# Graph attention over a sparse matrix: the second part's order on three engines written out by hand, and the last tile worked in column halves

## The chip, the core and the metric

The kernel runs on one core of a Trainium2 chip. The metric is the device time of one launch in microseconds (us); lower is better. The core's engines are named as the profile names them: PE (TensorE, the matrix array), DVE (VectorE), ACT (ScalarE), POOL (GpSimd) and SP (SyncE). Each works through a queue of its own in order, and waits there for semaphores that other engines or transfers raise.

## What is computed

```python
def reference(x, adj, Wf, bf, Wg, bg, W, bW):        # x: 3327 x 1024, adj: 3327 x 3327
    h = jnp.maximum(_layernorm(x, axis=-1), 0.0)
    f, g = h @ Wf + bf, h @ Wg + bg
    e = jax.nn.relu(f @ g.T)
    attention = softmax(jnp.where(adj > 0, e, NEG), axis=1)
    return x + attention @ (h @ W + bW)
```

All values are float32. Of each row of `adj` only some are set: a row has at most 37 neighbours in this data.

## The kernel before, in words

`edge_path` never builds the full score matrix. Its **first part** (to about 250 us) reads `adj` and `x`, stores h to memory (`hd`), makes a list of neighbours for every row (`pd`, and `cd` for rows with more than 24), and multiplies the two weight matrices into one, A. It sorts the rows by their number of neighbours and cuts them into 26 tiles of 128 rows.

The **second part** handles one tile after another, in the order `ORDER`. I call a tile by its *position* in that order, 0 to 25. `CAPS` gives each tile's cap, the number of neighbours that it is worked with. By position the caps are 12, 16, 37, 25, 23, 22, 21, 21, 20, 20, 19, 19, 18, 18, 17, 17, 17, 16, 15, 15, 15, 14, 14, 13, 13, 11. For one tile:

- `turned`, `taken`, `third`, `emptied` make q = h A. PE transposes the tile's rows of h (8 transposes), ACT copies them (`hT`), PE multiplies them by A in three thirds of 342 columns (16 passes each), and ACT copies each third into `q`; before that the banks are filled with a bias row on ACT. This is done two positions ahead.
- `dot`: for each neighbour k, POOL starts an indirect gather of 128 rows of `hd` into a buffer `G` (26 buffers in turn), and DVE multiplies G by q and sums it to a score (L986, 128x1024).
- `softmax`: DVE masks the scores (L995) and takes the negated maximum (L997; L999 joins it with that of an earlier chunk). ACT takes the exp (L1002). In a second chunk ACT makes a factor `al` (L1005) and scales the sum y by it (L1011); DVE joins the denominators (L1006) and inverts (L1009).
- `combine`: y is the sum of G times its weight. Some of the G go through DVE (L1052, one sum each, 128x1024). The others are scaled on ACT (L1046) and added by PE, transposed, in a PSUM tile `yT_ps` (L1026, 8 transposes of 128x128 each); `on_tensor` says which. The first G is scaled on ACT (L1050).
- `project`: PE adds y itself transposed (8 more), ACT copies the result (`yT`), PE multiplies by W (L1068, two halves of 512 columns, 32 passes).
- `result` and `finish`: ACT scales the product (L1090), POOL gathers the rows of x onto it and writes it out. The last tile's result is scaled and added on DVE (L1084).

Tiles with a cap over 16 are worked in two chunks, the first of 10 neighbours (19 at position 2); the others in one piece. While one unit is summed, dots of the next unit run: `AHEAD` of them are issued right after `softmax`, the rest when the next unit begins. `project` of a tile is put off until the next tile's first chunk has been combined; with a next tile in one piece, it comes at once.

What sets the order: the first part stands in a block `tc.manual_schedule` that keeps DVE, ACT, PE, POOL and SP in program order. In the second part the framework's scheduler chooses each engine's order by its own estimates, and `in_line` (L864) adds edges that keep certain PE and ACT instructions behind the last ones recorded in `queue`. DVE is free, except that the last tile's dots stand behind the sums of the tile before (`behind`).

`failed` (L1113) makes a flag of the checks of the first part: a 1x1 matmul and a DVE copy (L1120, L1121); all engines load the flag (L1122) and branch on it past a dense fallback that these inputs do not need. It is called when position 23 has been projected.

Of the kernel before, what the change touches and what calls it, by code (L numbers as in the profile page):

```python
# [33 lines left out]
AHEAD = 3  # L34
# [262 lines left out]
def edge_path(ctx: ExitStack, tc: tile.TileContext, x, adj, Wf, bf, Wg, bg, W, bW, out, flag):  # L297
# [563 lines left out]
    queue = {}  # L861

    @contextmanager
    def in_line():  # L864
        with ExitStack() as both:
            for ins in queue.values():
                both.enter_context(tc.issue_after(ins.ins))
            yield


# [15 lines left out]

    one = small.tile([P, 1], FP, name="one")
    tc.keep_in_program_order(nc.scalar.activation(one, ident[:, :1], AF.Exp))

    for at in range(2):  # L890
        filled(p_q, "ps_q", vb, QB, 6 + at, True)
        filled(p_o, "ps_o", bWb, CB, at, True)
# [15 lines left out]
    def turned(s):  # L908
# [3 lines left out]
        for g in range(0, KD, 4):  # L912
            ps = p_t.tile([P, 4, P], FP, name="ps_t")
            e["ps_t"].append(ps)
            with in_line():
                for k in range(4):
                    ins = nc.tensor.transpose(ps[:, k, :], e["hp"][:, (g + k) * P : (g + k + 1) * P], ident)  # L917
            queue["pe"] = ins

    def taken(s):  # L920
        e = st[s]
        for g, ps in enumerate(e["ps_t"]):
            with in_line():
                queue["act"] = nc.scalar.copy(e["hT"][:, 4 * g : 4 * g + 4, :], ps)  # L924

    def third(s, i):
# [7 lines left out]
        with in_line():  # L934
            for k in range(KD):
                ins = nc.tensor.matmul(  # L936
                    ps[:, :QB], e["hT"][:, k, :], A_sb[:, k, o : o + QB], start=False, stop=(k == KD - 1),
                    skip_group_check=True,
                )
        queue["pe"] = ins  # L940

    def emptied(s, i):
        e = st[s]
        at = 3 * ORDER.index(s) + i
        with in_line():
            ins = nc.scalar.copy(e["q"][:, i * QB : (i + 1) * QB], e["ps_q"][i][:, :QB])  # L946
            if at + 2 < 3 * NT:
                ins = filled(p_q, "ps_q", vb, QB, at + 2)
        queue["act"] = ins
# [29 lines left out]
    def dot(s, k, behind=None):  # L979
# [5 lines left out]
        with tc.issue_after(behind.ins) if behind else ExitStack():  # L985
            nc.vector.tensor_tensor_reduce(  # L986
                junk, g, e["q"][:, :D], 1.0, e["q"][:, D : D + 1], op0=ALU.mult, op1=ALU.add,
                accum_out=e["sc"][:, k : k + 1],
            )
# [247 lines left out]
```

## Time and profile before

| | us |
|---|---|
| median of 15 runs | 1317.32 |
| lowest and highest | 1308.71 and 1325.28 |
| the profiled execution | 1313.65 |
| its span, first to last instruction | 1311.7 |
| DVE busy in the span | 1158.1 |
| PE busy in the span | 1114.8 |
| ACT busy, POOL busy | 609.8, 886.6 |
| mean granted clock of PE | 0.942 |

A row of the table of groups gives line, engine, operation, output and inputs, count, then busy time and mean ns of one, then the idle time of the engine just before these instructions and what ended most of it. A row of a timeline gives start, length, engine, line, operation, tiles and shapes, and in brackets the idle time before it with what released it. A row of the waits gives who waited for whom, the total in us, how often, and the longest. A row of the chain of waits gives start, length and what the chain ran through. An instruction's length on DVE overlaps the next one's start slightly, so steps are best read from start to start.

### The profile page before, as it was taken

The page shows a single profiled execution, that of the slowest core. Times are in us where ns is not written, and L with a number is a line of the kernel's source. Part 1 is how long each engine was busy: PE and PEld are TensorE (multiplying, and loading weights), DVE is VectorE, ACT ScalarE, POOL GpSimd, SP SyncE. Part 2 cuts the span into 40 slices and gives each one's busy share as a digit, 9 for nine tenths or more (in the row PEclk, how much of TensorE's full clock was granted, in tenths as well). Part 3 has the DMA queues.
Part 4 walks back from the last instruction along what each step waited for, and adds up shares of the span by engine and source line. Part 5 has one row for each costly group of instructions (what it writes and reads, how often), then busy time and mean ns, then how long its engine had stood idle before and what let it go on. Part 6 is the DMA issues. An engine that isn't in the chain of part 4 may idle for free.

```text
span 1311.7 us, 14316 instructions
## 1 busy us (share of the span) xinstructions
PE 1114.8 (85%) x4488; PEld 702.2 (54%) x4488; DVE 1158.1 (88%) x2205; ACT 609.8 (46%) x943; POOL 886.6 (68%) x678
## 2 busy tenths in 40 slices
PE   2799962967846899999888998999999899999995
PEld 2566641643625566556555655556555556555553
DVE  6999987686899899999999999999999999999980
ACT  5899977133206356435543354443335433333350
POOL 8999974374675777777676676766665667656611
PEclk8899985977977999999999999999999899999998
DMA  9999995886787999989888888888888788888821
GB/s 370 413 395 397 397 338 190 275 307 252 231 297 238 318 298 312 332 294 308 286 302 264 299 292 288 283 280 287 277 291 268 241 275 283 262 286 303 271 69 50
DMA packets 101802, 374.44 MB, mean 285 GB/s; under 512 B 14747, under 2 KB 18490, under 8 KB 98519
## 3 DMA queue, kind: packets, MB, share of 16 engines
q0 software_dynamic: 80624, 290.96, 66.7%
q1 hardware_dynamic: 21094, 82.49, 16.6%
q8 instruction: 37, 0.61, 0.2%
q14 instruction: 47, 0.39, 0.1%
HBM read 344.11 MB, written 29.30 MB: 285 GB/s over the span
## 4 chain that ended last, share of the span: by engine, by line
DVE 29%; issue 29%; DMA 13%; PE 11%; ACT 8%; POOL 8%; another core or an unknown queue 2%; SPq 0%; POOLq 0%; DVEq 0%; ACTq 0%
DVE G L1052 12%; DVE cand L482 6%; POOL G L356 5%; DVE junk L986 5%; DMA G<-hd,pi 5%; PE ps_o L1068 4%; ACT G L1046 4%; PE yT_ps L1026 4%; DMA xt<-in_x_dram 3%; PE ps_q L936 3%; DMA G<-hd,perm 2%; POOL r L419 1%; DVE sc L986 1%; DVE held L493 1%
## 5 line engine op out<-in xcount | busy, mean ns | idle before, releaser
L356 POOL DMA_INDIRECT G<-hd,pi x454 | 538.1, 1185 | 206.1 <-issue 102.3
L986 DVE CUSTOM_DVE_ANT_0 junk<-G,q 128x1024 bf16<-128x1024 f32 x468 | 601.4, 1285 | 35.5 <-DMA G<-hd,pi 15.8
L1052 DVE SCALAR_TENSOR_TENSOR G<-G,sc 128x1024 f32<-128x1024 f32 x275 | 353.8, 1287 | 32.1 <-ACT G L1011 15.7
L1068 PE MATMUL ps_o<-W_sb,yT 128*128 128x512 f32 x832 | 364.0, 595 | 6.2 <-ACT yT L1060 6.2
L936 PE MATMUL ps_q<-A_sb,hT 128*128 128x342 f32 x1152 | 345.0, 454 | 9.5 <-issue 9.5
L936 PEld LDWEIGHTS ps_q<-A_sb,hT 128*128 128x128 f32 x1152 | 215.6, 191 | 117.5 <-issue 14.9
L1026 PE MATMUL yT_ps<-ident,G 128*128 128x128 f32 x1544 | 205.7, 285 | 85.7 <-ACT G L1046 61.9
L1068 PEld LDWEIGHTS ps_o<-W_sb,yT 128*128 128x128 f32 x832 | 157.7, 190 | 200.8 <-issue 188.5
L1026 PEld LDWEIGHTS yT_ps<-ident,G 128*128 128x128 f32 x1544 | 178.6, 147 | 116.2 <-ACT G L1046 74.8
L419 POOL TENSOR_TENSOR r<-r,iotaj 128x1664 f32<-128x1664 f32 (+3 forms) x50 | 183.8, 3726 | 12.5 <-ACT r L412 12.5
L1046 ACT ACTIVATE G<-G,sc 128x1024 f32<-128x1024 f32 x167 | 182.4, 1142 | 0.0
L1002 ACT ACTIVATE sc<-sc,nm 128x10 f32<-128x10 f32 (+11 forms) x41 | 12.5, 304 | 342.7 <-DVE nm L999 252.1
L552 PE MATMUL ps_A<-WgT,WfT 128*128 128x342 f32 x432 | 130.9, 462 | 2.5 <-ACT WfT L547 2.5
L482 DVE MAX8 cand<-r 128x8 f32<-128x208 f32 (+2 forms) x416 | 119.1, 360 | 4.1 <-POOL r L419 3.3
L552 PEld LDWEIGHTS ps_A<-WgT,WfT 128*128 128x128 f32 x432 | 81.9, 193 | 43.1 <-ACT WfT L547 2.6
L946 ACT COPY q<-ps_q 128x342 f32<-128x342 f32 x72 | 31.4, 437 | 155.3 <-PE ps_q L936 114.3
L412 ACT ACTIVATE r<-r 128x3327 f32<-128x3327 int32 (+3 forms) x27 | 77.3, 2863 | 8.1 <-DMA r<-in_adj_dram 8.1
L1102 POOL DMA_INDIRECT out_dram<-res,perm x25 | 31.9, 1276 | 65.2 <-DMA res<-in_x_dram,perm 61.0
L356 POOL DMA_INDIRECT res<-in_x_dram,perm x25 | 41.9, 1674 | 47.0 <-ACT res L1090 37.9
L924 ACT COPY hT<-ps_t 128x512 f32<-128x512 f32 x48 | 25.4, 581 | 75.7 <-PE ps_t L917 55.1
L356 POOL DMA_INDIRECT pi<-pd,perm x26 | 29.0, 1116 | 34.7 <-DMA cd<-cand 17.7
L536 PE MATMUL ps_tr<-ident,A_sb 128*128 128x128 f32 x128 | 22.5, 334 | 27.5 <-DMA A_sb<-in_L_gnn_Wg_dram 23.5
(139 smaller groups left out, 713.3 us busy)
## 6 DMA issues: line engine op xcount, KB each, us to landing
r<-in_adj_dram SPq DMA_DIRECT2D x24, 1663.5 KB, 12.2
xt<-in_x_dram SPq DMA_DIRECT2D x25, 512.0 KB, 12.9
hd<-xt SPq DMA_DIRECT2D x25, 512.0 KB, 10.5
G<-hd,pi POOLq DMA_INDIRECT x454
A_sb<-in_L_gnn_Wg_dram SPq DMA_DIRECT2D x8, 512.0 KB, 17.3
A_sb<-in_L_gnn_Wf_dram SPq DMA_DIRECT2D x8, 512.0 KB, 11.4
W_sb<-in_L_gnn_W_dram POOLq DMA_DIRECT2D x1, 4096.0 KB
cd<-cand SPq DMA_DIRECT2D x25, 64.0 KB, 11.8
```

What stands on the lines that cost most here:

```text
L356: return nc.gpsimd.indirect_dma_start(out=to, out_offset=None, in_=table, in_offset=bass.IndirectOffsetOnAxis(ap=idx, axis=0), **kw,)
L412: nc.scalar.activation(r[:n, b:e], a[:n, b:e], AF.Sign, accum_out=to)
L419: eng.tensor_mul(r[:n, b:e], r[:n, b:e], iotaj[:n, b:e])
L482: nc.vector.max(cands[t][:n, s * 8 : s * 8 + 8], r[:n, s * SW : min(N, (s + 1) * SW)])
L552: nc.tensor.matmul(ps[:, :QB], WfTs[c][:, k, :], WgT[:, k, o : o + QB], start=(k == 0), stop=(k == KD - 1))
L936: ins = nc.tensor.matmul(ps[:, :QB], e["hT"][:, k, :], A_sb[:, k, o : o + QB], start=False, stop=(k == KD - 1), skip_group_check=True,)
L986: nc.vector.tensor_tensor_reduce(junk, g, e["q"][:, :D], 1.0, e["q"][:, D : D + 1], op0=ALU.mult, op1=ALU.add, accum_out=e["sc"][:, k : k ...
L1026: ins = nc.tensor.matmul(e["yT"][:, c, :], g[:, c * P : (c + 1) * P], ident, is_transpose=True, start=(first and c % 4 == 0), stop=(last a ...
L1046: queue["act"] = nc.scalar.activation(g, g, AF.Copy, scale=p)
L1052: e["summed"] = nc.vector.scalar_tensor_tensor(y, g, p, y, op0=ALU.mult, op1=ALU.add)
L1068: ins = nc.tensor.matmul(ps, yT[:, k, :], W_sb[:, k, o * CB : (o + 1) * CB], start=False, stop=(k == KD - 1), skip_group_check=True,)
L1102: ins = nc.gpsimd.indirect_dma_start(out=out[:, :], out_offset=bass.IndirectOffsetOnAxis(ap=perm[:, s : s + 1] if s < N // P else final, a ...
```

## The change

The scheduler's choice in the second part is replaced: the whole second part stands in a `manual_schedule` block for ACT, DVE and PE, so each of these engines runs its instructions in program order; POOL and SP are still scheduled. `in_line`, `queue` and `behind` go.

The program order itself is new. After `softmax` of a unit come `AHEAD` = 2 dots of the next unit (none after positions 0 and 1), then `totalled` (the denominators and the inverse, formerly in `softmax`). In `combine` every DVE sum is followed by one dot of the next unit while there are any (`between`); after position 24's sums none is. Remaining dots come when the next unit begins. On ACT the factor `al` now comes ahead of the exp, and y is scaled within `softmax`, ahead of `emptied(…, 2)`, the copy of the last third of a coming q. Position 24 gives PE three of its G instead of six, position 25 five instead of four. `failed` keeps its place in the program, behind `project` of position 23; the flag is loaded after the last but one result's write.

The last tile goes through the new `ended`: its G for PE are scaled and transposed; then, for each half of 512 columns, DVE scales the first G and adds the others (six instructions of 128x512), PE adds this half of y transposed, ACT copies the half, and PE runs the half of the W product that reads it.

```diff
 LARGEST = 16
-AHEAD = 3
+AHEAD = 2
 LAG = 2
...
-    queue = {}
-
-    @contextmanager
-    def in_line():
-        with ExitStack() as both:
-            for ins in queue.values():
-                both.enter_context(tc.issue_after(ins.ins))
-            yield
-
...
-        with in_line():
-            ins = nc.scalar.copy(e["q"][:, i * QB : (i + 1) * QB], e["ps_q"][i][:, :QB])
-            if at + 2 < 3 * NT:
-                ins = filled(p_q, "ps_q", vb, QB, at + 2)
-        queue["act"] = ins
+        nc.scalar.copy(e["q"][:, i * QB : (i + 1) * QB], e["ps_q"][i][:, :QB])
+        if at + 2 < 3 * NT:
+            filled(p_q, "ps_q", vb, QB, at + 2)
...
-    def dot(s, k, behind=None):
+    def dot(s, k):
         e = st[s]
         g = G[s, k] = gpool.tile([P, D], FP, name="G")
         with tc.issue_after(st["gate"].ins) if s == ORDER[1] else ExitStack():
             st["gathered"] = gather(g, hd[:, :], e["edges"][k])
         junk = jpool.tile([P, D], BF, name="junk")
-        with tc.issue_after(behind.ins) if behind else ExitStack():
-            nc.vector.tensor_tensor_reduce(
-                junk, g, e["q"][:, :D], 1.0, e["q"][:, D : D + 1], op0=ALU.mult, op1=ALU.add,
-                accum_out=e["sc"][:, k : k + 1],
-            )
-
-    def softmax(s, k0, k1, last):
+        nc.vector.tensor_tensor_reduce(
+            junk, g, e["q"][:, :D], 1.0, e["q"][:, D : D + 1], op0=ALU.mult, op1=ALU.add,
+            accum_out=e["sc"][:, k : k + 1],
+        )
+
+    def softmax(s, k0, k1):
 
         e = st[s]
         sc = e["sc"][:, k0:k1]
         nc.vector.scalar_tensor_tensor(sc, sc, 0.0, e["mask"][:, k0:k1], op0=ALU.max, op1=ALU.add)
         nm = small.tile([P, 1], FP, name="nm")
         nc.vector.tensor_reduce(nm, sc, AX.X, ALU.max, negate=True)
+        l = small.tile([P, 1], FP, name="l")
         if k0:
             nc.vector.tensor_tensor(nm, nm, e["nm"], op=ALU.min)
-        l = small.tile([P, 1], FP, name="l")
-        with in_line():
-            nc.scalar.activation(sc, sc, AF.Exp, bias=nm, accum_out=l)
+            e["al"] = small.tile([P, 1], FP, name="al")
+            nc.scalar.activation(e["al"], e["nm"], AF.Exp, bias=nm, scale=-1.0)
+        nc.scalar.activation(sc, sc, AF.Exp, bias=nm, accum_out=l)
         if k0:
-            al = small.tile([P, 1], FP, name="al")
-            nc.scalar.activation(al, e["nm"], AF.Exp, bias=nm, scale=-1.0)
-            nc.vector.scalar_tensor_tensor(l, e["l"], al, l, op0=ALU.mult, op1=ALU.add)
+            nc.scalar.activation(e["y"], e["y"], AF.Copy, scale=e["al"])
+        else:
+            e["y"] = G[s, 0]
+            if s != ORDER[-1]:
+                nc.scalar.activation(e["y"], e["y"], AF.Copy, scale=e["sc"][:, :1])
+        e["nm"] = nm
+        e["ls"] = (e.get("l"), l)
+        e["l"] = l
+
+    def totalled(s, k0, last):
+        e = st[s]
+        if k0:
+            before, l = e["ls"]
+            nc.vector.scalar_tensor_tensor(l, before, e["al"], l, op0=ALU.mult, op1=ALU.add)
         if last:
             e["rs"] = small.tile([P, 1], FP, name="rs")
-            nc.vector.reciprocal(e["rs"], l)
-        if k0:
-            queue["act"] = nc.scalar.activation(e["y"], e["y"], AF.Copy, scale=al)
-        e["nm"], e["l"] = nm, l
+            nc.vector.reciprocal(e["rs"], e["l"])
...
 
     def on_tensor(s, k0, k1):
 
 
-        m = min(max(0, CAPS[s] - (7 if s in ORDER[-2:] else 12)), k1 - k0 - 2) if s not in ORDER[:2] else (k1 - k0) // 2
+        if s in ORDER[:2]:
+            m = (k1 - k0) // 2
+        elif s in ORDER[-2:]:
+            m = {ORDER[-2]: 3, ORDER[-1]: 5}[s]
+        else:
+            m = min(max(0, CAPS[s] - 12), k1 - k0 - 2)
         ks = range(max(k0, 1), k1)
         return [k for i, k in enumerate(ks) if (i + 1) * m // len(ks) > i * m // len(ks)]
+
+    def transposed_into(e, g, c, first, last):
+        nc.tensor.matmul(
+            e["yT"][:, c, :], g[:, c * P : (c + 1) * P], ident, is_transpose=True,
+            start=first, stop=last, skip_group_check=True,
+        )
...
-    def combine(s, k0, k1, last, ahead=None):
+            transposed_into(e, g, c, first and c % 4 == 0, last and c % 4 == 3)
+
+    def combine(s, k0, k1, last, ahead, between):
         e = st[s]
-        if not k0:
-            e["y"] = G[s, 0]
         y = e["y"]
         e["first"] = True
         pe = on_tensor(s, k0, k1) if last else []
-        for k in range(k0, k1):
+        for k in range(max(k0, 1), k1):
             p = e["sc"][:, k : k + 1]
             g = G[s, k]
             if k in pe:
                 if k == pe[-1] and ahead is not None:
                     taken(ahead)
-                with in_line() if k == pe[-1] else ExitStack():
-                    queue["act"] = nc.scalar.activation(g, g, AF.Copy, scale=p)
-                queue["pe"] = sum_transposed(e, g, e["first"], False)
+                nc.scalar.activation(g, g, AF.Copy, scale=p)
+                sum_transposed(e, g, e["first"], False)
                 e["first"] = False
-            elif k == 0:
-                queue["act"] = nc.scalar.activation(y, y, AF.Copy, scale=p)
             else:
-                e["summed"] = nc.vector.scalar_tensor_tensor(y, g, p, y, op0=ALU.mult, op1=ALU.add)
+                nc.vector.scalar_tensor_tensor(y, g, p, y, op0=ALU.mult, op1=ALU.add)
+                between()
+
+    def ended(s, k1):
+        e = st[s]
+        y = e["y"]
+        pe = on_tensor(s, 0, k1)
+        yT = yTpool.tile([P, KD, P], FP, name="yT")
+        e["yT"] = p_y.tile([P, KD, P], FP, name="yT_ps")
+        e["o"] = [banks.pop(("ps_o", OH * (NT - 1) + o)) for o in range(OH)]
+        for i, k in enumerate(pe):
+            nc.scalar.activation(G[s, k], G[s, k], AF.Copy, scale=e["sc"][:, k : k + 1])
+            for c in range(KD):
+                transposed_into(e, G[s, k], c, not i and c % 4 == 0, False)
+        for g in range(0, KD, 4):
+            half = slice(g * P, (g + 4) * P)
+            nc.vector.tensor_scalar(y[:, half], y[:, half], e["sc"][:, :1], None, op0=ALU.mult)
+            for k in range(1, k1):
+                if k not in pe:
+                    nc.vector.scalar_tensor_tensor(
+                        y[:, half], G[s, k][:, half], e["sc"][:, k : k + 1], y[:, half], op0=ALU.mult, op1=ALU.add
+                    )
+            for c in range(g, g + 4):
+                transposed_into(e, y, c, False, c % 4 == 3)
+            nc.scalar.copy(yT[:, g : g + 4, :], e["yT"][:, g : g + 4, :])
+            for o, ps in enumerate(e["o"]):
+                for k in range(g, g + 4):
+                    nc.tensor.matmul(
+                        ps, yT[:, k, :], W_sb[:, k, o * CB : (o + 1) * CB], start=False, stop=(k == KD - 1),
+                        skip_group_check=True,
+                    )
...
@@ -1119,7 +1130,6 @@
         ps = p_t.tile([P, 4, P], FP, name="ps_t")[:, 0, :]
         nc.tensor.matmul(ps[0:1, 0:1], worst, onesf, start=True, stop=True)
         nc.vector.tensor_copy(flag[0:1, 0:1], ps[0:1, 0:1])
-        return nc.values_load(flag[0:1, 0:1], min_val=0, max_val=1 << 20)
 
...
-
-                dot(s, k, st[ORDER[-2]].get("summed") if s == ORDER[-1] else None)
...
+    with tc.manual_schedule(engines={
+        mybir.EngineType.Activation, mybir.EngineType.DVE, mybir.EngineType.PE
+    }):
+        one = small.tile([P, 1], FP, name="one")
+        nc.scalar.activation(one, ident[:, :1], AF.Exp)
+        for at in range(2):
+            filled(p_q, "ps_q", vb, QB, 6 + at, True)
+            filled(p_o, "ps_o", bWb, CB, at, True)
...
+        for i, (s, k0, k1) in enumerate(units):
+            last = k1 == CAPS[s]
+            at = ORDER.index(s)
+            s2, a, b = units[i + 1] if i + 1 < len(units) else (s, 0, 0)
+            ahead = ORDER[at + 2] if last and at + 2 < NT else None
+            if at and ahead is not None:
+                fetch(ahead)
...
+            softmax(s, k0, k1)
+            if late:
+                emptied(late.pop(), 2)
+            covered = AHEAD if i > 1 else 0
+            dots(s2, range(a, min(b, a + covered)))
+            totalled(s, k0, last)
...
+            if ahead is not None:
+                turned(ahead)
+            coming = iter(range(a + covered, b) if i > 1 and s != ORDER[-2] else ())
+
+            def between(s2=s2, coming=coming):
+                for k in coming:
+                    dots(s2, [k])
+                    break
+
+            if s == ORDER[-1]:
                 result(ORDER[at - 1])
+                ended(s, k1)
                 done_with.append(ORDER[at - 1])
+                break
+            combine(s, k0, k1, last, ahead, between)
...
+                if at + 2 == NT - 1:
+                    failed()
+        finish(done_with.pop())
+        bad = nc.values_load(flag[0:1, 0:1], min_val=0, max_val=1 << 20)
+        result(ORDER[-1])
+        finish(ORDER[-1])
     return bad
```

## The prediction

> **What bounds the kernel now.** I read the shares per engine, the windows, the waits, the timelines and the chain of waits. N(p) is the moment when VectorE ends the negated maximum that closes position p (L999, or L997 for a tile in one piece); dots are L986, sums L1052.
>
> ```profile
> PE 1114.8 (85%) x4488; PEld 702.2 (54%) x4488; DVE 1158.1 (88%) x2205; ACT 609.8 (46%) x943; POOL 886.6 (68%) x678
> L986 DVE CUSTOM_DVE_ANT_0 junk<-G,q 128x1024 bf16<-128x1024 f32 x468 | 601.4, 1285 | 35.5 <-DMA G<-hd,pi 15.8
> L1052 DVE SCALAR_TENSOR_TENSOR G<-G,sc 128x1024 f32<-128x1024 f32 x275 | 353.8, 1287 | 32.1 <-ACT G L1011 15.7
> ```
>
> From 251 us on, 468 dots and 275 sums fill VectorE. TensorE is almost as full: in 1100 to 1200 us it is busy 97.0 us of 100, VectorE 95.3. So VectorE's gaps are worth something only while TensorE keeps up. Those gaps, by the waits from 400 to 1244 us (total, times, longest):
>
> ```profile
> DVE G L1052 <- ACT G L1011: 15.7, 10, 1.7
> DVE G L1052 <- issue: 8.9, 7, 1.7
> DVE l L1006 <- ACT al L1005: 5.2, 8, 0.7
> DVE G L1052 <- ACT G L1050: 4.9, 5, 1.0
> ```
>
> All waits of that view add up to 41 us, 37.9 of them on ScalarE at the ends of tiles; the change reaches for them. How one arises, on ScalarE at position 11 (N = 797.8):
>
> ```profile
> 797.82 0.30 ACT L1002 ACTIVATE sc<-sc,nm 128x9 f32<-128x9 f32 x1 [17.76 <-DVE G L1052]
> 798.02 0.18 ACT L1002 ACTIVATION_READ_ACCUMULATOR sc<-sc,nm 128x1 f32 x1
> 798.12 0.28 ACT L1005 ACTIVATE al<-nm 128x1 f32<-128x1 f32 x1
> 798.30 1.13 ACT L1046 ACTIVATE G<-G,sc 128x1024 f32<-128x1024 f32 x1
> 799.34 1.13 ACT L1011 ACTIVATE G<-G,al 128x1024 f32<-128x1024 f32 x1
> 800.38 0.42 ACT L946 COPY q<-ps_q 128x342 f32<-128x342 f32 x1
> ```
>
> The sum on VectorE starts at 800.51, when y is scaled; and the last third of the next tile's q comes only after it. From about 1206 us the chain of waits runs through TensorE to the end:
>
> ```profile
> 1239.22 0.87 PE yT_ps L1026 x8
> 1240.10 4.60 PE ps_q L936 x16
> 1244.70 13.73 PE ps_o L1068 x32
> 1258.43 6.13 PE yT_ps L1026 x56
> 1264.58 0.59 ACT yT L1060
> 1265.22 14.00 PE ps_o L1068 x32
> 1279.22 4.38 PE yT_ps L1026 x40
> 1283.62 0.59 ACT yT L1060
> 1284.26 14.02 PE ps_o L1068 x32
> ```
>
> VectorE has finished its sums by 1277.5 and waits 14 us for the product.
>
> **Prices.** Start to start on VectorE: dot to dot 1.33, dot to sum 1.205, sum to dot 1.20, sum to sum 1.31 (six took 7.89), a small operation 0.1 to 0.2. ScalarE: scaling a G 1.05, copying a q third 0.45. TensorE: eight transposes 0.87, a q third 4.6, a W product 13.75.
>
> **1. The two covering dots.** After N(p) the changed order puts two dots of the next tile ahead of L1006, L1009 and the sums. At a tile's end these read the next q, whose last third stands on ScalarE behind the two exps and the scaling of y: 0.2 + 0.3 + 1.05 + 0.45 + 0.05 = 2.05 us of idle VectorE, where now a sum starts after 2.7 with L1006 and L1009 done in the gap. So nothing is covered; the gap changes place. (After a first chunk the dots read a q that is there, and they do cover.) One changed cycle up to the first sum of the next first chunk: 2.05, two dots 2.54, two small 0.37, sum dot sum 3.6, seven dots 9.31, softmax 0.31, two dots 2.54 = 20.7. Then pairs at 2.405, what is left of nine sums or of the dots, and small operations 0.74. By cap: 25: 48.4 (now 51.0, distances of N), 23: 45.8 (47.2), 22: 44.4 (45.0), 21: 43.1 (43.4, 43.5), 20: 41.9 (42.3, 42.2), 19: 40.8 (41.1, 40.9), 18: 39.7 (38.5 twice), 17: 38.6 (36.1, 37.15, 37.1), and 16 in one piece 26.3 (28.85). The short tiles lose since their sums now stand in a row and hide no small operation. Sum -1.1 (-4 to +3: some two small operations a cycle may cost 0.1 more or less).
>
> **2. First-chunk sums of long tiles.** ScalarE runs in order: the first chunk's exp stands behind all G scalings of the tile before and the copy of the first q third, which waits for TensorE. TensorE begins the thirds at N + 21.0, 19.9, 16.5, 14.7 at positions 2 to 5 (rows at 422.17, 472.12, 515.88, 559.08). Third 4.65, copy and refill 0.9, exp and scaling 1.6: the sum can start 7.15 later, at 28.2, 27.05, 23.65, 21.85. VectorE wants it at 20.7 and has nothing else in line: 7.5 + 6.3 + 2.9 + 1.1, and 0.1 twice: **+18.0**. Now further dots stand ahead of that sum, and the gaps there are 1.1, 1.1 and 0.9. Bounds: 3.1, what these gaps cost now, and 20.
>
> **3. Tiles in one piece (positions 17 to 24).** The eleven sums alternate with the next tile's dots, so the last sum ends 28.0 after the first dot (2.65 + 10 x 2.405 + 1.28). Then TensorE transposes y (0.93), makes the last q third (4.77) and ScalarE copies it; with hand-overs 6.3 us, as from the sum's end at 1206.79 to a possible copied q at 1213.0. Only then may the next dots start: 34.3 us a cycle at every cap up to 15. Now the cycles are 35.3, 34.4, 32.7, 33.3, 31.7, 31.8: sums come earlier, and late dots cover the third. First dots of position 24: N(17) + 2.0 + 6 x 34.3 = 207.8; last sum of 23 at 235.8; transposes, third and product 19.4 more: position 23's W product ends at N(17) + 255.2, now 1258.3 - 1014.0 = 244.3. **+10.9** (0 to 14).
>
> **4. The tail,** from the end of that product, now 40.0 us to the end of the last W product. The flag's 1x1 matmul (now at 1227.39) stands behind that product, and VectorE's copy of it stands ahead of position 24's softmax: VectorE is idle some 18 us, and all that is left of its work, to the last tile's sums, is queued behind. Then flag and softmax 0.85, exp, scaling, q 2.0, two dots 2.6, nine sums (three of 12 stay on TensorE instead of six) 11.8: 17.3. TensorE idles for them. Nine dots 12.0, softmax and exp 0.9: 30.1. Meanwhile y's transposes and position 24's product: 17.35 + 2.0 + 0.65 + 16.4 = 36.4. The last tile's five scalings stand behind the two copies of that product: 36.4 + 1.6 + 5.3 = 43.3; transposes 0.9; half of y 0.5, copy 0.7, half a product 6.9, again 0.5, 0.7, 6.9: 60.4. **+20.4.** The twelve half sums on VectorE (8.4 us by 0.70, between half of 1.28 and the 0.75 of the 128x512 row L1084) end at 38.6 and are covered. Bounds: 13, with TensorE at full clock and scalings that need not wait for the product; 23, with the last product at half clock too.
>
> The 2.0 and the 16.4 are rows after idle: 8 transposes at 402.92 took 1.97 instead of 1.04 after 27.2 us of idle, a product 16.40 instead of 13.89 after 4.9. The Trainium skill (TensorE: Matmul & The Clock Gate, "What's actually happening") has the array at half clock after about 3.4 us idle until it has been busy as long; an estimate from that page is 1.7 us of loss for this product instead of 2.5, which would make the sum 0.8 less. It speaks against the change, since the flag makes such an idle stretch.
>
> **5. Start.** No dots between the sums of positions 0 and 1; the 10.4 us gap before 317.8 takes seven sums, but ScalarE's exp waits for y's copies until 313.8, so sums run 315.4 to 324.6. One gather more stands ahead of the residual gather on POOL (13 for 12), which spares a late dot. N(2) at 398.8 instead of 401.2: -2.4 (-4 to +1.3; the upper end is the table load, 1.28, now next to the first exp).
>
> POOL's gathers keep their 26 buffers. In a one-piece cycle the residual's gather and write hold POOL until about 26 us; then it issues seven gathers (1.25 each) before the next dots, and three stand already, so I take nothing. If that lead is gone, a dot waits up to 5.8 us, as at 343.6 after the gather issued at 337.8.
>
> **Sum:** -2.4 - 1.1 + 18.0 + 10.9 + 20.4 = +45.8. The profiled execution took 1313.65 (span 1311.7), 3.7 below the median of 1317.32: 1359.4. I take 1358.
>
> **Rivals.** *The tail alone:* if between tiles the waits stay as large as now (parts 1 to 3 nothing; for it: TensorE's 97%), 1313.65 - 2.4 + 20.4 = 1332. *Faster:* the covering dots do cover. It is decided at ScalarE behind N: if the last q third lies ready before y is scaled, the 37.9 us of waits at tile ends go, and the half product saves 6.9 at the end: 1313.65 - 37.9 - 6.9 = 1269, or less far where TensorE holds it. Against it: the order on ScalarE, the same in every tile. *Worse:* late gathers or a half clock beyond the tail: part 2 at 20, part 3 at 14, part 4 at 23, and 8 us of gathers: 1375 and more. *No effect:* parts cancel; the order does change, so this is only chance.
>
> **Chances.** Forecast 0.70 (own range 1342 to 1372), tail alone 0.14, worse 0.06, faster 0.07, no effect 0.03. The range 1326 to 1373 takes in the first two. About 0.3% is what a measurement can tell from no change: faster 0.07, same 0.03, slower 0.90.
>
> **What would show it.** Right: dots waiting some 2 us on the q copy at each tile end; a sum waiting about 7 us after N(2); one-piece cycles of 34 us; one VectorE wait of 15 to 18 us on the flag's matmul; TensorE idle before position 24's y. Wrong: dots that follow N(p) without a gap, or a flag copy that does not wait.

## The result and the profile after

The changed kernel takes 1377.93 us (median of 9 runs, 1374.78 to 1384.47), the kernel before 1316.41 (47 runs): a ratio of 1.0469, 95% interval 1.0442 to 1.0497. The forecast was 1358 with a range to 1373: the direction was right, the loss too small. The profiled executions lie further apart than the medians (1384.28 us, 6.4 above the changed kernel's median, and 1313.65, 2.8 below the other's). Their spans are 1382.5 us against 1311.7: +70.8, where the forecast's sum was +45.8.

From the page of the changed kernel, busy time by engine and the two large groups of VectorE (L961 is the dot, L1038 the sum):

```profile
PE 1128.8 (82%) x4472; PEld 721.8 (52%) x4472; DVE 1164.3 (84%) x2214; ACT 608.8 (44%) x940; POOL 888.6 (64%) x678
L961 DVE CUSTOM_DVE_ANT_0 junk<-G,q 128x1024 bf16<-128x1024 f32 x468 | 601.3, 1285 | 71.7 <-ACT q L923 44.1
L1038 DVE SCALAR_TENSOR_TENSOR G<-G,sc 128x1024 f32<-128x1024 f32 x272 | 349.7, 1286 | 40.8 <-ACT G L984 39.6
```

The same work at the same price (1285 and 1286 ns), and VectorE's share falls from 88% to 84%. So the loss is idle time of VectorE. VectorE's waits from 400 to 1330 us (total, times, longest):

```profile
DVE junk L961 <- ACT q L923: 44.1, 18, 4.8
DVE G L1038 <- ACT G L984: 37.5, 7, 12.2
DVE flag L1132 <- PE ps_t L1131: 18.1, 1, 18.1
```

These are three of the forecast's parts: dots behind the q copy, sums of a first chunk behind its scaled y, the flag. How the first arises, on ScalarE at position 11 (N = 828.4):

```profile
828.41 0.29 ACT L977 ACTIVATE al<-nm 128x1 f32<-128x1 f32 x1 [17.94 <-DVE nm L975]
828.61 0.29 ACT L978 ACTIVATE sc<-sc,nm 128x9 f32<-128x9 f32 x1
...
828.90 1.13 ACT L980 ACTIVATE G<-G,al 128x1024 f32<-128x1024 f32 x1
829.93 0.42 ACT L923 COPY q<-ps_q 128x342 f32<-128x342 f32 x1
830.39 0.45 ACT L874 COPY ps_q<-vb 128x342 f32<-128x342 f32 x1
830.77 3.23 ACT L1034 ACTIVATE G<-G,sc 128x1024 f32<-128x1024 f32 x3
```

The q copy that the covering dots need is fourth in line; they start at 830.39, 2.0 after N. The first scaled G, which TensorE needs, is now sixth: before, it was third (798.30 after N = 797.8). The chain of waits at the end (start, length, what):

```profile
1294.70 13.73 PE ps_o L1082 x32
...
1310.54 0.43 ACT q L923
...
1325.50 1.98 PE yT_ps L1011 x8
1327.50 0.59 ACT yT L1075
1328.14 16.06 PE ps_o L1082 x32
1344.22 0.69 ACT res L1102
...
1345.63 1.08 ACT G L1049
1346.76 5.70 PE yT_ps L1011 x44
1352.48 0.59 ACT yT L1062
1353.12 7.13 PE ps_o L1065 x16
...
1361.37 7.15 PE ps_o L1065 x16
```

Between position 23's product and y of 24, where TensorE had gone on at once, the chain now leaves TensorE for 17 us. Cut by stage, three pairs of profiles, changed kernel less kernel before, in us. The second and third pair come from the experiments: one chip on which TensorE had pauses (stretches of idle time for which the profile names no releaser, explained below), as in the first profiles, and one on which it had none.

| stretch | forecast | first profiles | second pair with pauses | pair without pauses |
|---|---|---|---|---|
| up to N(2) | -2.4 | -1.6 | -8.3 | +4.0 |
| N(2) to N(17) | +16.9 | +37.9 | +32.5 | +21.1 |
| N(17) to the end of position 23's product | +10.9 | +13.7 | +12.3 | +13.9 |
| from there to the end of the last product | +20.4 | +20.2 | +19.8 | +20.2 |
| rest | 0 | +0.6 | +0.7 | +0.9 |
| sum | +45.8 | +70.8 | +57.0 | +60.1 |

In two groups of runs the kernel before took 1315.7 and 1316.4 us, in four others 1294.7 to 1297.1. Each of the later groups ran on one chip, so below this is called the chip's, though it may be the hour's. Ratios are to the kernel before of the same group; spans are compared only between profiles of the same kind.

### The profile page after: what moved, and what is told of

Read it like the earlier page. It is cut to its first block, busy times and chain, and to the rows that moved or that the text cites. A ratio compares the mean times of both kernels' runs of the same rounds, so it can differ in the third digit from the quotient of the medians.

```text
span 1382.5 us, 14268 instructions
## 1 busy us (share of the span) xinstructions
PE 1128.8 (82%) x4472; PEld 721.8 (52%) x4472; DVE 1164.3 (84%) x2214; ACT 608.8 (44%) x940; POOL 888.6 (64%) x678
## 4 chain that ended last, share of the span: by engine, by line
DVE 28%; issue 26%; PE 15%; DMA 12%; POOL 10%; ACT 7%; another core or an unknown queue 0%; SPq 0%; POOLq 0%; DVEq 0%; ACTq 0%
DVE G L1038 15%; POOL G L356 7%; PE yT_ps L1011 6%; DVE junk L961 5%; DMA G<-hd,pi 4%; DMA xt<-in_x_dram 4%; PE ps_q L915 4%; DVE cand L482 4%; PE ps_o L1082 3%; POOL r L419 2%; ACT G L1034 2%; DMA res<-in_x_dram,perm 2%; DVE sc L961 1%; PE ps_o L1065 1%; DMA cd<-cand 1%
## 5 line engine op out<-in xcount | busy, mean ns | idle before, releaser
L356 POOL DMA_INDIRECT G<-hd,pi x454 | 528.7, 1165 | 238.1 <-issue 105.8
L961 DVE CUSTOM_DVE_ANT_0 junk<-G,q 128x1024 bf16<-128x1024 f32 x468 | 601.3, 1285 | 71.7 <-ACT q L923 44.1
L1038 DVE SCALAR_TENSOR_TENSOR G<-G,sc 128x1024 f32<-128x1024 f32 x272 | 349.7, 1286 | 40.8 <-ACT G L984 39.6
L1082 PE MATMUL ps_o<-W_sb,yT 128*128 128x512 f32 x800 | 353.2, 599 | 16.0 <-issue 11.9
L1011 PE MATMUL yT_ps<-ident,G 128*128 128x128 f32 x1528 | 214.6, 301 | 120.6 <-ACT G L1034 77.1
L1011 PEld LDWEIGHTS yT_ps<-ident,G 128*128 128x128 f32 x1528 | 195.0, 157 | 144.0 <-ACT G L1034 87.6
L1082 PEld LDWEIGHTS ps_o<-W_sb,yT 128*128 128x128 f32 x800 | 153.0, 192 | 205.5 <-issue 195.8
L1034 ACT ACTIVATE G<-G,sc 128x1024 f32<-128x1024 f32 x160 | 171.7, 1140 | 0.0
L977 ACT ACTIVATE al<-nm 128x1 f32<-128x1 f32 x15 | 4.4, 294 | 303.0 <-DVE nm L975 233.3
L899 PE MATMUL ps_t<-ident,G 128*128 128x128 f32 x192 | 26.7, 285 | 26.2 <-DMA G<-hd,perm 26.2
## 6 DMA issues: line engine op xcount, KB each, us to landing
cd<-cand SPq DMA_DIRECT2D x25, 64.0 KB, 12.2
```

Source lines behind the costliest of these rows:

```text
L356: return nc.gpsimd.indirect_dma_start(out=to, out_offset=None, in_=table, in_offset=bass.IndirectOffsetOnAxis(ap=idx, axis=0), **kw,)
L961: nc.vector.tensor_tensor_reduce(junk, g, e["q"][:, :D], 1.0, e["q"][:, D : D + 1], op0=ALU.mult, op1=ALU.add, accum_out=e["sc"][:, k : k ...
L1011: nc.tensor.matmul(e["yT"][:, c, :], g[:, c * P : (c + 1) * P], ident, is_transpose=True, start=first, stop=last, skip_group_check=True,)
L1034: nc.scalar.activation(g, g, AF.Copy, scale=p)
L1038: nc.vector.scalar_tensor_tensor(y, g, p, y, op0=ALU.mult, op1=ALU.add)
L1082: nc.tensor.matmul(ps, yT[:, k, :], W_sb[:, k, o * CB : (o + 1) * CB], start=False, stop=(k == KD - 1), skip_group_check=True,)
```

## The experiments

**One edit each (before: 1296.5 us here).** The changed kernel itself was not run on this chip. On three others of that kind its spans were 1351.9, 1352.9 and 1348.4 us; gains of span below are against the first of these, so they are good to some 4 us.

First chunk's exp ahead of the copy of the first q third:

```diff
                     third(ahead, 0)
-                    emptied(ahead, 0)
                     third(ahead, 1)
+                    if at and units[i + 1][2] != CAPS[units[i + 1][0]]:
+                        behind.append(ahead)
+                    else:
+                        emptied(ahead, 0)
...
             softmax(s, k0, k1)
+            if behind:
+                emptied(behind.pop(), 0)
```

> Only ScalarE's order is changed: the exp of a first chunk stands ahead of the copy of the next q's first third, which waits for TensorE. Theory A (the first chunk's exp behind that copy is what cost 37.5 us, twice the forecast, and TensorE's idle time at those tiles only follows from it): the seven waits of VectorE's sums on the scaled y (37.5 us in all) fall below 4 us, N(2) to N(17) goes from 650.8 to 610 to 616 us, and the time from 1378 to 1338 to 1346. Theory B (TensorE itself is late at these tiles, at half clock and short of instructions, and VectorE must wait for it somewhere): the wait moves to the dots or to the next tile's end, N(2) to N(17) stays above 630 and the time above 1358.

1339.81 us, 1.0328 (1.0298 to 1.0357). In its waits of VectorE from 400 us on

```profile
DVE G L1038 <- ACT G L984: 4.1, 2, 3.6
```

is all that is left of the sums' wait: the place is right. But N(2) to N(17) took 618.7 us and the gain was 15 us of span, not 37: on chips of this kind the waits were only 17.0 in the unchanged kernel. That raised the question of the pauses. POOL's gathers moved by a place or two in the scheduler's order, here and in the third and fourth edit.

The flag ahead of position 23's projection:

```diff
+                if at + 2 == NT - 1:
+                    failed()
                 if not at or i + 1 == len(units) or units[i + 1][2] == CAPS[units[i + 1][0]]:
                     rest()
                     rest = None
-                if at + 2 == NT - 1:
-                    failed()
```

> The flag's reduction, matmul and copy stand ahead of the W product of position 23 on TensorE instead of behind it. Theory A (the flag is what empties the tail): the one wait of 18.1 us on VectorE goes, the end of position 23's product to the end of the last product goes from 60.1 to about 41 us (24 G transposes 2.7, y 0.9, copy 0.7, product 13.8, two result copies 1.6, five scalings 5.3, transposes 0.9, halves 15.3), the time from 1378 to 1357 to 1362. Theory B (VectorE's wait is covered by TensorE, which makes the product of 24 anyway, and the last tile's five scalings behind its copies set the end): under 8 us gained, 1370 or more.

1340.40 us, 1.0324 (1.029 to 1.0358). The 18 us wait is gone and product to product took 43.5 us instead of 60. But the flag's matmul now waits 3.2 us for VectorE ahead of the last q third, the dots of position 24 wait 7.1 for that q, and position 23's product ends 3.2 later after N(23). 11 us of span gained.

The copy of the last q third ahead of the exps:

```diff
+            if late:
+                emptied(late.pop(), 2)
             softmax(s, k0, k1)
-            if late:
-                emptied(late.pop(), 2)
```

> On ScalarE the copy of the last q third stands ahead of the two exps and of the scaling of y at every tile end. Theory A (the covering dots wait only for ScalarE's order): the fifteen waits of 2.0 us at the ends of tiles in two chunks go; where TensorE's thirds come late the first chunk's sum then waits that much longer (positions 2 to 10, thirds from N + 11.7 or later), so of 30 us some 15 to 25 stay gained: 1353 to 1363. In tiles in one piece the wait stays, since the third itself is made late. Theory B (TensorE sets the pace of every cycle): VectorE's waits change place, and less than 8 us is gained: 1370 or more.

1325.48 us, 1.0217 (1.0188 to 1.0245): the largest single term, 30 us of span.

```profile
DVE G L1038 <- ACT G L984: 26.5, 8, 8.9
...
DVE junk L961 <- ACT q L923: 16.9, 6, 4.6
```

The dots' wait, N(2) included, fell from 48.9 (first such profile of the unchanged kernel) to 16.9, the first-chunk sums' rose from 17.0 to 26.5: part of the wait moved, as expected, and the rest was gain. The scaled G comes 0.85 earlier too (TensorE's first transpose at N + 2.75, not 3.60). Theory B falls: TensorE did not set the pace.

The last third ahead of y's transposes:

```diff
+        if then is not None:
+            third(then, 2)
         sum_transposed(e, e["y"], e["first"], True)
         for g in range(0, KD, 4):
             nc.scalar.copy(yT[:, g : g + 4, :], e["yT"][:, g : g + 4, :])
-        if then is not None:
-            third(then, 2)
```

> TensorE makes the next q's last third ahead of y's transposes instead of behind them. Theory A (in a one-piece tile the sums, y's transposes, the third, the copy and the dots are one chain of 34.2 us): the waits of 2 to 4.8 us on the q copy at positions 17 to 24 fall to the 2.0 that ScalarE's order costs or less, the cycles from 34.2 to between 31.8 (VectorE's own work) and 32.5, and the time from 1378 to 1360 to 1366. Theory B (TensorE is full there, 31 to 32 us of work in each cycle, and the gain goes into waits for it): cycles above 33.5, 1371 or more.

1346.62 us, 1.0381 (1.0351 to 1.0412). The one-piece cycles became 34.3 three times, then 32.9, 33.0, 31.7: N(17) to N(23) 200.6 us instead of 206.0. The chain existed: every wait of the dots at positions 17 to 22 is now 1.98 us, what ScalarE's order costs. But three cycles stayed at 34.3 without it, since VectorE's own work in these is 32.2 us, not 31.8; so theory A explains about half.

**Whole end, all four edits, and both kernels (before: 1315.7 us here).** e5 replaces the half sums, transposes and products of the last tile by whole ones.

> The changed kernel with the last tile's sums, y's transposes and W product whole again, all else as changed. Theory A (the halves come too late to pay: VectorE's half sums are long done when the last scaled G has been transposed, so the halves only put a copy between two half products): end of the G transposes to the end of the last product falls from 16.2 us (0.5 + 0.7 + 7.1, twice, less overlap) to 15.4 (0.9 + 0.65 + 13.8), time 0 to 1.5 us lower than the changed kernel's. Theory B (the halves save most of half a product, 6.9): 4 to 7 us more.

> The changed kernel, unchanged. Theory A (the forecast's sum of 18.0 us for the first-chunk sums was right for TensorE without pauses, and the 37.5 of the first profile came from pauses of 2.6 to 3.9 us and the half clock that follows): on a chip where before takes 1297 us and shows no pauses, those waits are 17 to 19 us, and the profiled span is 48 to 56 us above that of the kernel before. Theory B (the excess is the change's own): waits of 35 us or more, and a span 65 us or more above.

e5: 1369.87 us, 1.0413 (1.0372 to 1.0454); the changed kernel beside it 1369.97, 1.0422 (1.0378 to 1.0466). End of product 23 to end of the last product: 59.0 whole, 59.7 in halves. The halves bring nothing; that they cost 0.7 rests on one profile each.

> The kernel before, unchanged, beside the changed kernel on one chip. Where the first four experiments ran, it took 1296.5 us instead of 1316.4, and TensorE had none of the pauses (rows that wait for issue) that both first profiles show around 293 to 309, 416, 468 and 513 us. Theory A (the pauses belong to a chip or a spell, not to the kernel): where its time is near 1297, N(1) to N(2) is about 83 us instead of 93.9 and the pauses after N(2) to N(4), 1.2 to 1.8 us a tile before, are under 0.3. Theory B (they belong to the program): they are there again.

The kernel before had its pauses again (1.3, 2.1 and 0.3 us behind N(2) to N(4)), span 1309.8; the changed kernel 3.4, 3.8 and 0, first-chunk waits 31.7 us, span 1366.8: +57.0. That lies between the two theories on the changed kernel; theory A's own case, a chip without pauses, came later: waits of 17.0 us, as it says, but a span 60.1 above, where it has 48 to 56.

> All four edits together: first chunk's exp ahead of the q copy, the flag ahead of position 23's product, the last q third's copy ahead of the exps, the last third ahead of y's transposes. Theory A (the four are separate terms of VectorE's idle time, and TensorE has room): the gains add up, some 17 + 17 + 31 + 10 of the changed kernel's time, so 1275 to 1290 where before takes 1297, the dots follow N without a gap, and the changed kernel's idea (two covering dots) then pays. Theory B (TensorE, over 95% busy in the kernel before, sets the cycle): the gains overlap, and the time stays at 1297 or above.

1293.91 us, 0.9823 (0.9777 to 0.9869): faster than both kernels. It is 76 us below the changed kernel beside it, where the four gains were to add up to 75; the times expected for a chip on which the kernel before takes 1297 us were not put to the test. This chip had pauses, 1.9, 0 and 2.8 us behind N(2) to N(4), and yet the first-chunk sums waited only 5.5 us, where the changed kernel beside it waited 31.7. From cap 23 down to cap 18 every cycle is 0.7 to 2.3 us shorter than in the kernel before at its side, at cap 17 between 0.6 shorter and 0.4 longer: the covering dots do pay once their q is there. What is left in its tail:

```profile
1228.41 1.28 DVE L961 CUSTOM_DVE_ANT_0 junk<-G,q 128x1024 bf16<-128x1024 f32 x1 [8.11 <-ACT q L923]
```

This is the flag again, as in e2: its matmul, waiting for VectorE, stands ahead of the third.

**Are the pauses the cause?** TensorE behind N(2) in the first profile of the changed kernel, N = 399.6 (idle before and its releaser in brackets):

```profile
413.75 1.26 PE L1011 MATMUL yT_ps<-ident,G 128*128 128x128 f32 x10
415.23 0.42 PE L1011 MATMUL yT_ps<-ident,G 128*128 128x128 f32 x2 [0.22 <-issue]
416.66 0.53 PE L1011 MATMUL yT_ps<-ident,G 128*128 128x128 f32 x3 [1.00 <-issue]
418.07 0.38 PE L1011 MATMUL yT_ps<-ident,G 128*128 128x128 f32 x2 [0.88 <-issue]
419.51 0.49 PE L1011 MATMUL yT_ps<-ident,G 128*128 128x128 f32 x3 [1.06 <-issue]
420.26 5.10 PE L1011 MATMUL yT_ps<-ident,G 128*128 128x128 f32 x30 [0.25 <-issue]
425.20 9.08 PE L915 MATMUL ps_q<-A_sb,hT 128*128 128x342 f32 x31
```

Two or three matmuls every 1.4 us, with transposes that were ready; the granted clock then drops (0.5 from 420.9 to 424.3) and 30 transposes take 5.1 us. The thirds begin at N + 25.6. Without pauses, N = 389.3 (this chip's profile of the changed kernel):

```profile
402.73 5.81 PE L1011 MATMUL yT_ps<-ident,G 128*128 128x128 f32 x49
409.44 1.09 PE L1011 MATMUL yT_ps<-ident,G 128*128 128x128 f32 x8 [0.91 <-ACT G L1034]
410.37 9.37 PE L915 MATMUL ps_q<-A_sb,hT 128*128 128x342 f32 x32
```

The thirds begin at N + 21.1. To see whether TensorE's idle time and half clock bring the pauses, TensorE fills the idle time ahead of positions 2 to 7 with more of the transposes of the fetched rows:

```diff
             for k in range(4):
-                nc.tensor.transpose(ps[:, k, :], e["hp"][:, (g + k) * P : (g + k + 1) * P], ident)
+                for _ in range(1 + WARM.get(ORDER.index(s) - 2, 0)):
+                    nc.tensor.transpose(ps[:, k, :], e["hp"][:, (g + k) * P : (g + k + 1) * P], ident)
```

> The kernel before, unchanged, beside the next three on one chip: its N(2) and its pauses on TensorE are what the start of the changed kernel is to be measured against. If the pauses (stretches in which TensorE runs a pair of instructions every 0.7 us and waits for nothing that the profile shows) belong to the chip, the kernel takes 1295 to 1300 us where they are missing, with N(2) near 385 us, and 1310 to 1320 where they are there, with N(2) near 400.

> The changed kernel, unchanged, as the standard for the next one. With pauses behind N(2) and N(3) of more than 2 us each: first-chunk waits of 30 us or more. Without: 17 to 19.

> The changed kernel, in which TensorE fills its idle time ahead of positions 2 to 7 by transposing the fetched rows 9, 7, 5, 4, 2 and 3 times more (the same values to the same place), so that it comes to the scaled G at full clock. Theory A (VectorE's wait idles TensorE, the half clock makes it late, it then runs without a break and the pauses follow): half clock in the 32 us after N(2) to N(4) falls from 7 to 15 us to under 4, the thirds start at N + 21, 18 and 16, pauses under 0.5, first-chunk waits 16 to 19 us where the unchanged kernel has 30 or more. Theory B (the pauses come whatever the clock was): the waits stay within 5 us of the unchanged kernel's on the same chip.

The kernel before: span 1291.8, no pauses, N(2) at 385.3. The changed kernel: span 1351.9, no pauses, waits

```profile
DVE G L1038 <- ACT G L984: 17.0, 6, 7.7
```

With fillers: 1352.45 us, 1.0424 (1.0401 to 1.0448); half clock in the 32 us behind N(2) to N(4) 3.4, 0 and 0 us instead of 7.8, 9.6 and 6.8; thirds at N + 21.09 instead of 21.10; waits (lines shifted by 3)

```profile
DVE G L1041 <- ACT G L987: 16.9, 6, 7.7
```

So the half clock alone costs nothing there: ScalarE's scalings, 1.05 us apart, set the pace, and TensorE has caught up with them before the thirds. The kernel with fillers ran twice more beside the unchanged one, for the question of the pauses:

> The fillers ahead of positions 2 to 7 once more, since no pauses came in the kernel with fillers and in the standard beside it. Theory A (where pauses come, they come because TensorE was idle, fell to half clock and then runs its backlog of transposes without a break): with the fillers TensorE keeps pace with ScalarE, pauses behind N(2) to N(4) under 0.5 us each and first-chunk waits of 16 to 19 us, where the unchanged kernel beside it has 2 to 4 us and 30 or more. Theory B (pauses come whatever the clock): waits within 5 us of the unchanged kernel's. If the kernel beside it has no pauses, this tells nothing new.

> The fillers a third time, for a chip on which the unchanged kernel beside it shows pauses. Theory A: pauses under 0.5 us each behind N(2) to N(4), waits 16 to 19 us. Theory B: waits within 5 us of the unchanged kernel's. Without pauses beside it, it tells nothing new.

No pauses in any of these four profiles (waits 17.0, 17.0 and 16.8, 16.8; e8 1.0419, 1.0396 to 1.0443; e9 1.0443, 1.0422 to 1.0464). Whether the change's idle time makes the pauses longer, from 1.3 to 2.1 us behind N(2) and N(3) before to 3.4 to 3.9 in both such profiles of the changed kernel and 2.4 to 2.9 in that of e5, stays open.

Two things in the traces at hand narrow it. Pauses come at full clock too: behind N(4) there are 1.2 us of them in the first profile of before and 2.8 in that of all four edits, with a granted clock of 1.00 for 50 us ahead. And they are not TensorE's alone. ScalarE in the first profile of the changed kernel, and the thirds and transposes on TensorE that it copies:

```profile
287.74 9.37 PE L915 MATMUL ps_q<-A_sb,hT 128*128 128x342 f32 x32
296.95 1.04 PE L1011 MATMUL yT_ps<-ident,G 128*128 128x128 f32 x8
...
306.70 0.44 ACT L923 COPY q<-ps_q 128x342 f32<-128x342 f32 x1 [9.08 <-issue]
...
313.83 1.07 ACT L1075 COPY yT<-yT_ps 128x512 f32<-128x512 f32 x2 [6.21 <-remote]
```

The second third was made by 297.1 and y was transposed by 298.0, but ScalarE copies them 9.6 and 15.8 us later and idles 9.1 and 6.2 us in between ("remote" is a release that the profile can put down to no instruction). Without pauses the two copies start at 296.21 and 297.08, as soon as TensorE is done.

**The version that beats both.** All four edits, the flag at the start of the second part, ScalarE's last scalings ahead of the result copies, the end whole (c2); then the flag at position 12 instead (c3, run twice).

```diff
-                result(ORDER[at - 1])
-                ended(s, k1)
+                ended(s, k1, lambda: result(ORDER[at - 1]))
...
+            if at == 12 and last:
+                failed()
             softmax(s, k0, k1)
```

> The four edits with the flag made once at the start, where its inputs are ready, instead of ahead of position 23's product, the last tile's scalings ahead of the result copies on ScalarE, and its end whole. Theory A (the flag's matmul, waiting for VectorE ahead of the third, still cost 8.1 us of VectorE's time in the kernel with all four edits; the scalings 4.3): the wait of 8.1 us on the q copy in the tail goes, and the time is 8 to 13 us below that kernel's, a ratio to the kernel before of 0.970 to 0.977. Theory B (TensorE's two products set the tail anyway): within 4 us of it, 0.979 or more.

> As the version with the flag at the start, but the flag is made at position 12, just ahead of its last softmax. Theory A (the flag at the start held up TensorE's fills and the first scores: N(0) was 281.2 us instead of 274.8): N(0) back to 274 to 277, 5 to 6.5 us less, a ratio to the kernel before of 0.984 to 0.988 where it takes 1297, of 0.965 to 0.975 where it takes 1316. Theory B (the first scores wait for the gathers, whatever the flag does): N(0) within 1.5 us of 281, no gain.

> The version with the flag at position 12 once more: where the kernel before takes about 1316 us, a ratio of 0.965 to 0.980 to it, since the kernel with all four edits had 0.9823 there; where it takes 1297, 0.988 to 0.993 as measured.

c2: 1285.23 us, 0.9914 (0.9894 to 0.9935). The tail's wait of 8.1 is gone, but N(0) went from 274.8 to 281.2. TensorE's fills are not held up (264.47, against 265.39 in the changed kernel); VectorE is. The flag's copy stands ahead of the first dots and waits for its matmul, which stands behind the first part's products:

```profile
264.58 0.14 DVE L1130 CAST flag<-ps_t 1x1 int32<-1x1 f32 x1 [19.85 <-PE ps_t L1129]
```

The first dot starts at 264.95 instead of 256.58. c2's ratio expectation was made from the other kind of chip, where the kernel before loses more, and says little. c3: 1283.99, 0.9904 (0.9886 to 0.9921), and again 1282.72, 0.9911 (0.9892 to 0.9929): N(0) back at 274.5, but of the 5 to 6.5 us expected only 2.9 of span were gained, on another chip and with overlapping intervals, since at position 12 VectorE waits for the flag:

```profile
DVE flag L1130 <- PE ps_t L1129: 3.3, 1, 3.3
```

No place tried for it was free. Neither version was run on a chip with pauses.

## Why the forecast was wrong

**Part 1, the covering dots: right.** They waited 2.0 us at each of 15 two-chunk tile ends, for the reason named; e3 gave the price of that order, some 30 us. Cycle lengths without the first-chunk waits: forecast 611.7 us from N(2) to N(17) (the sum of its caps), measured 650.7 - 37.5 = 613.2 in the first profile and 630.5 - 17.0 = 613.5 without pauses.

**Part 2, the first-chunk sums: here it failed.** The place was right (e1), the size not: 37.5 us instead of 18.0 in the first profile, 31.7 in the second with pauses. The step that failed is "TensorE begins the thirds at N + 21.0, 19.9, 16.5, 14.7 ... Third 4.65": these were rows of the kernel before, carried over as if pauses would delay the changed kernel no more than it. In the changed kernel they began at N + 25.6, 23.8, 17.1 and 14.9, and the first third, to ScalarE's copy of it, took 4.8, 6.5, 8.0 and 5.3 us. With these the forecast's own sum gives waits of 12.2, 12.0, 6.9 and 2.0 us, where it had 7.5, 6.3, 2.9 and 1.1. At position 6 a wait of 2.9, where it had 0.1, is ScalarE's: the third ends at 632.9 and is copied at 635.5. Without pauses the rows do carry over: the thirds begin at 21.0, 17.8, 15.8, 14.7 in the kernel before and at 21.1, 18.0, 15.9, 14.8 in the changed kernel, though it has more half clock there (7.8, 9.6 and 6.8 us behind N(2) to N(4) against 5.8, 0 and 0), and the waits are 17.0. The forecast's upper bound of 20 came from the same rows and so was none, while the trace of before did show TensorE pausing, at 293 to 309 us (one matmul of a third every 1.4 to 2.1 us) and 1.4 and 1.8 us long behind N(2) and N(3); these rows were not weighed. What the runs show is that the excess appears only with pauses, and that with the first chunk's exp ahead of the copy (and the other three edits) pauses bring no more than 5.5 us of these waits; what makes the pauses is not shown.

**Part 3, one-piece tiles: 3 us small, and right in part by chance.** From first dots to first dots the cycles were 37.3, twice 34.3 and three times 34.2, where 34.3 was forecast. But the chain that was forecast sets only the first and the last three, whose dots wait 3.3 to 4.8 us for it. In the other two it is hidden: VectorE's own work, 32.2 us, and the 2.0 of ScalarE's order happen to make 34.3 as well. The first was long because TensorE idled 4.5 us ahead of y of position 17 and did its transposes and third at half clock (1.97 and 6.9 us instead of 0.9 and 4.6). The half clock was priced in the tail and not here, though the trace of before has it at the same place (1.97 and 5.75).

**Part 4, the tail: right.** 60.1 us from product to product against 60.4; the flag's wait 18.1 against some 18; position 24's product 16.05 against 16.4. The estimate worked out from the Trainium skill (TensorE: Matmul & The Clock Gate, "What's actually happening"), 1.7 us lost to the half clock, stood against the forecast's 2.5: measured 16.05 - 13.89 = 2.2 behind 9.1 us of idle, with a granted clock of 0.5 in the product's first 4.2 us.

**Part 5, the start: right by chance.** -1.6 us in the first profiles, -8.3 in the second pair with pauses, +4.0 without. The 10.4 us wait at 317.8 that the seven sums were to fill is there only with pauses: in the profile of the kernel before without them no wait on q between 300 and 400 us is listed, so there is nothing to fill. Where the other run of before had pauses:

```profile
DVE junk L986 <- ACT q L946: 9.1, 1, 9.1
```

So even without pauses the loss, +60.1 us of span, is 14.3 above the forecast's sum: 6.4 of it at the start, 4.2 between N(2) and N(17), where the kernel before is itself 3.5 us faster without its pauses (609.3 against 612.8), and 3.0 in part 3.

**The rivals.** "The tail alone" falls with N(2) to N(17). "Faster" put 6.9 us on the half product; e5 shows that the halves save nothing. In the changed kernel the last tile's scalings on ScalarE end at 1350.9 and its half sums at 1347.0, so the sums were not what the product waited for. Its other half holds: with the q copy ahead, the dots cover, and the combined version is faster. "Worse" named its 1375 and more from half clock and late gathers; the time came out there, but gathers cost VectorE at most 2.0 us in all behind 400 us, and the excess came with the pauses, which it did not name.

## What to carry to other kernels

An operation put in to cover a wait covers it only if its own operands stand ahead of that wait on the other engine: look up their place in that engine's order first. A start time taken from a profile carries that profile's pauses: where its rows wait for nothing that the profile names, the new order may pay more for them, so take the bound from the worst such row, or from a second profile elsewhere, and not from the row in place. A small flag in an in-order queue holds up what stands behind it: a wait of 18.1 us, one of 8.1 (3.5 at the same place without it), a start 6.4 later, a wait of 3.3.

## What the runs showed of the hardware

- On some chips TensorE has stretches with a few instructions every 0.7 or 1.4 us and no releaser in the profile; on others none, with the same program. In the kernel before they lie at 288 to 309 us and from about 15 us behind N(2) and N(3) on; in the changed kernel there are none of TensorE's at 285 to 312 us in the first profile, and ScalarE stands still there instead. The kernel before spans 1309.8 to 1311.7 us with pauses and 1291.8 without, and N(1) to N(2) makes some 14 of the difference (93.6 and 94.0 against 79.3). The DMA share is 1.00 at 285 to 309 us with pauses and 1.00 there without, so that alone does not explain them; nor does half clock, since they come at a granted clock of 1.00 too.
- Half clock behind an idle stretch costs nothing where another engine sets the pace (e7: 4 to 10 us less of it a tile, waits 17.0 and 16.9), and 2.2 us in a product that is on the path.
